# Two weight matrices turned by VectorE through DRAM, rows broadcast by DMA, and batch 0's projections in seven block products

## The chip, the cores and the metric

One core of one Trainium2 chip. The metric is the device time of one execution in microseconds (us). The engines are TensorE (PE, with its weight loads PEld), VectorE (DVE), ScalarE (ACT), GpSimd (POOL) and SyncE (SP, which here only issues DMAs). All data is float32. Each engine works through its own instructions in order and meets the others at semaphores.

## The reference

Sixteen batches of a graph with 1024 nodes and 256 channels pass two layers, each on the normalized and rectified input, with a residual:

```python
# layer 0
h = relu(layernorm(x))
c_adj = mean(h, axis=-1)                        # one value per node
A_s = 1 - |tanh((c_adj[m] - c_adj[n]) / 2)|     # the reference's A_s, in short
g = relu((h^T @ (adj * A_s)) * para)            # queries, 4 heads of 64
k, v = split(h @ kv_w)                          # kv_w: 256 x 512
x = x + softmax(q k^T * scale) @ v
# layer 1
h = relu(layernorm(x))
A_hat = (adj + I) * dinv[:, None] * dinv[None, :]   # dinv = rsqrt(degree)
z = batchnorm_relu((A_hat @ h) @ W1.T + b1)         # W1: 512 x 256
x = x + batchnorm(z @ W2.T + b2)                    # W2: 256 x 512
```

Both batchnorms take their statistics over all batches and nodes, so the second linear layer can only start when all sixteen batches have passed the first.

## The kernel before

[...] Wherever it can, the kernel forms a product of 2 x 2 blocks in seven block products instead of eight: sums of blocks are prepared, seven products are made, and the results are gathered by copies (ACT) and adds (DVE) out of PSUM.

The first stage runs batch by batch: `graph` (the weighted adjacency times h, then queries, keys and values), `attention` (four steps, each of scores, exponentials, sums and values), and then layer 1's aggregation and first linear product of the batch. Preparation of later batches is woven between by lists of steps: `between[c]` is called before block c of the graph, `hooks[s]` at the end of step s of attention. The order of PE, ACT, DVE, POOL and SP is the order of the program: a manual schedule. A DMA issued from SP or POOL waits in that engine's line like any other instruction.

PSUM is three double banks (`ps_s`) and two single ones (`ps_o`, `ps_t`). While a graph runs, two of the three double banks hold its sums (`gps`), and the third serves what is woven in. In attention `ps_o` holds the step's output; DVE turns it out of the bank (L874), and only then can the next step's values begin.

What lies around the change:

- Batch 0 and batch 1 use `graph` (plain products); from batch 2 on `graph_seven` is used, whose keys and values go through a class `Seven` in an order written out by hand. Its operands are sums of kv_w's blocks (made once by `make_key_sums`, stored in `kvs_d`, loaded for each batch) and sums of the turned h's blocks (`kt1` to `kt4`).
- Batch 0's h is turned by `turn_h` on SP's queue: DVE turns 32x32 blocks (L381), 32 small DMAs put them in place (L388).
- `prepare_row(b)` broadcasts batch b's sums of h over all partitions: by PE transposes for batches 0 and 1, through DRAM from batch 2 on (L310, L311).
- W1 is loaded with one DMA (L1408), turned by eight PE transposes (`turned`, L1378) and copied by ACT (L1412) into `w1T`, in `between[2]` of batch 0. `make_w1_sums` (L1095 to L1099) comes after batch 0's graph, then `make_key_sums`, `prepare_row(1)` and `diagonal`: POOL multiplies the diagonal blocks with the identity and adds it (L1348, L1349), and DVE reduces the products (L1350). Then comes attention of batch 0.
- The degree's row sums (L1335) run on ACT in `between[7]` and `between[8]` of batch 0; the column sums in the hooks of attention. `roots` (L1353 to L1355) makes `dinv`, `roots_row` (L1361, L1362) broadcasts it by PE transposes in `between[3]` of batch 1, and `scale_adj` (L1369) scales the turned adjacency with it: three rows in `between[4]`, one more behind it, four after the graph.
- W2 is loaded at the start of batch 15's attention (L1475), turned by eight PE transposes between its linear products (L1556) and copied by ACT (L1559).
- The pool `pp` has eight buffers with the tag "p". Exponentials of a step take all eight; the sums of W1, the diagonal's products, turned h and turned weights take one each while they live.

Of the kernel before, what the change touches and what calls it, by code (L numbers as in the profile page):

```python
# [10 lines left out]
F32 = mybir.dt.float32  # L11
# [6 lines left out]
P = 128  # L18
# [11 lines left out]
def fast_path(  # L30
# [37 lines left out]
    gs_d = [dram.tile([P, 4 * NC // 2, P], F32, tag=f"fgs_{b}", name=f"fgs_{b}") for b in range(B)]  # L68
    w1s_d = dram.tile([P, 4, FC * P // 2], F32, tag="fw1s", name="fw1s")
# [106 lines left out]
    with ExitStack() as stage:  # L176
# [126 lines left out]
        def prepare_row(b):  # L303
# [5 lines left out]
            if b > 1:  # L309
                nc.sync.dma_start(row_d[b].rearrange("(c p) -> p c", p=P), sums_of[b])  # L310
                nc.sync.dma_start(row, row_d[b].unsqueeze(0).to_broadcast([P, N]))  # L311
                return
# [6 lines left out]
            if b > 0:  # L319
                nc.scalar.copy(row, first)  # L320
                return


# [69 lines left out]

        def graph(b, between):
# [38 lines left out]
            for step in between.get("late", ()):  # L433
                step()
            for d in range(CC):
# [73 lines left out]
        def graph_seven(b, left, norm, load_more, last):  # L509
# [149 lines left out]
            t23 = ow.tile([P, 2, 512], F32, tag="sums", name=f"f_kt23_{b}")  # L659
            kt4 = pp.tile([P, 2, 512], F32, tag="acc", name=f"f_kt4_{b}", bufs=2)[:, 0]  # L660
            kt2, kt3 = t23[:, 0], t23[:, 1]
            part = lambda k, j: hT[k][:, ts(j, 512)]
            nc.vector.tensor_sub(kt3, part(1, 1), part(0, 1))
            nc.vector.tensor_add(kt2, kt3, part(0, 0))
            kt1 = part(0, 1)
            nc.vector.tensor_sub(kt1, kt1, part(0, 0))
            nc.vector.tensor_sub(kt4, part(1, 0), kt2)
# [10 lines left out]
            class Seven:  # L678


                def __init__(self, name, n, c, turned):
                    self.name, self.n, self.c, self.turned, self.ps = name, n, c, turned, {}
                    sums, o = (ps_s, "s"), (ps_o, "o")
                    self.banks = {
                        "x": sums,
                        2: (ps_t, "t"),
                        7: o if turned else sums,
                        4: sums if turned else o,
                    }

                def place(self, key, pool, tag):
                    ps = pool.tile([P, 512], F32, tag=tag, name=f"f_{self.name}ps{key}_{b}")
                    self.ps[key] = ps.rearrange("p (n q) -> p n q", n=4) if self.turned else ps

                def product(self, m):
                    w = lambda i, k: kvw_t[:, k, ts(2 * self.n + i, P)]
                    s = lambda q: sums[:, self.n, q]
                    left, right = {
                        1: (w(0, 0), part(0, 0)),
                        2: (w(0, 1), part(1, 0)),  # L700
                        3: (s(3), part(1, 1)),
                        4: (w(1, 1), kt4),
                        5: (s(0), kt1),
                        6: (s(1), kt2),
                        7: (s(2), kt3),
                    }[m]
                    more = m in (3, 5, 6)
                    key = "x" if more or m == 1 else m
                    if not more:
                        self.place(key, *self.banks[key])  # L710
                    ps = self.ps[key]
                    if not self.turned:
                        nc.tensor.matmul(  # L713
                            ps, left, right, start=not more, stop=True, skip_group_check=more
                        )
                        return
                    for n in range(4):
                        nc.tensor.matmul(  # L718
                            ps[:, n],
                            right[:, ts(n, P)],  # L720
                            left,
                            start=not more and n == 0,
                            stop=n == 3,
                            skip_group_check=True,
                        )

                def copy(self, i, j):
                    nc.scalar.copy(self.c(i, j), self.ps["x"])

                def add(self, i, j, m):  # L730
                    nc.vector.tensor_add(self.c(i, j), self.c(i, j), self.ps[m])  # L731

            V = Seven("v", 1, lambda i, j: v[:, 4 * j : 4 * j + 4, ts(i, P)], True)
            K = Seven("k", 0, lambda i, j: kT[:, i, ts(j, 512)], False)
# [366 lines left out]
        def make_key_sums():  # L1101
# [9 lines left out]
            nc.sync.dma_start(kvs_d, t)  # L1111

# [244 lines left out]
        def roots_row():  # L1357
            t = pp.tile([P, N], F32, tag="p", name="f_drow")
            ps = ps_s.tile([P, NC, P], F32, tag="s", name="f_drowps")
            for c in range(NC):  # L1360
                nc.tensor.transpose(ps[:, c, :], dinv[:, c : c + 1].to_broadcast([P, P]), ident)  # L1361
            nc.scalar.copy(  # L1362
                t.rearrange("p (i c q) -> p c i q", i=NC, c=NC),
                ps.rearrange("p c (q i) -> p c i q", i=NC),
            )
            drow.append(t)

        def scale_adj(m):
            nc.vector.scalar_tensor_tensor(  # L1369
                ahatT[:, m, :], ahatT[:, m, :], dinv[:, m : m + 1], drow[0], ALU.mult, ALU.mult  # L1370
            )

        def turned(src, n, k, name):

            ps = ps_s.tile([P, k, n, P], F32, tag="s", name=f"f_{name}ps")
            for d in range(k):
                for f in range(n):
                    nc.tensor.transpose(ps[:, d, f, :], src[:, f, ts(d, P)], ident)  # L1378
            return ps.rearrange("p d f q -> p (d f q)")

        with tc.manual_schedule(engines={ENG.PE, ENG.Activation, ENG.DVE, ENG.Pool, ENG.SP}):
# [25 lines left out]
            w1n = w4.tile([P, FC, C], F32, tag="w4", name="f_w1n")  # L1407
            nc.sync.dma_start(w1n, W1.rearrange("(f p) d -> p f d", p=P))  # L1408
            w1T = big.tile([P, CC, F1], F32, tag="w1T", name="f_w1T")

            def turn_w1():
                nc.scalar.copy(w1T.rearrange("p d f -> p (d f)"), turned(w1n, FC, CC, "w1"))  # L1412
# [13 lines left out]
                        turn_w1,  # L1426
# [13 lines left out]
                        lambda: place_adj_aside(6, nc.vector.tensor_copy),  # L1440
                    ],
# [4 lines left out]
                    6: [lambda: prepare_end(1), lambda: again(0)],  # L1446
                    7: [lambda m=m: row_sums(m) for m in range(4)],
                    8: [lambda m=m: row_sums(m) for m in range(4, NC)],
# [3 lines left out]
            make_key_sums()  # L1452
            prepare_row(1)
            diagonal()
            for b in range(B):

                hooks, aside, behind = {}, {}, None
                if b + 1 < B:
# [9 lines left out]
                    if b == 0:  # L1468
                        for m in range(NC):
                            hooks.setdefault(m // 2, []).append(lambda m=m: column_sums(m))  # L1470
                        hooks[3].append(roots)
# [989 lines left out]
```

## Time and profile before

| | |
|---|---|
| median of 3 runs | 2368.37 us (2367.6 to 2368.43) |
| the profiled execution | 2368.14 us, span 2366.4 us |
| TensorE's granted clock in it | 0.997 |
| batch 0: graph, then keys and values | 15.91 to 50.67, then to 64.45 us |
| batch 0: attention | 65.41 to 121.82 us |
| batch 1: graph, then keys and values | 121.75 to 150.20, then to 165.29 us |

The page gives the busy time of each engine, the span in slices, the chain of work that ended last, and the costliest groups. A timeline lists an engine's instructions: start, duration, engine, line, operation, what is written and read, how often, and in brackets how long the engine was idle before and what released it. A list of waits gives total time, times and the longest.

### The profile page before, as it was taken

The page shows a single profiled execution, that of the slowest core. Times are in us where ns is not written, and L with a number is a line of the kernel's source. Part 1 is how long each engine was busy: PE and PEld are TensorE (multiplying, and loading weights), DVE is VectorE, ACT ScalarE, POOL GpSimd, SP SyncE. Part 2 cuts the span into 40 slices and gives each one's busy share as a digit, 9 for nine tenths or more (in the row PEclk, how much of TensorE's full clock was granted, in tenths as well). Part 3 has the DMA queues.
Part 4 walks back from the last instruction along what each step waited for, and adds up shares of the span by engine and source line. Part 5 has one row for each costly group of instructions (what it writes and reads, how often), then busy time and mean ns, then how long its engine had stood idle before and what let it go on. Part 6 is the DMA issues. An engine that isn't in the chain of part 4 may idle for free.

```text
span 2366.4 us, 25724 instructions
## 1 busy us (share of the span) xinstructions
PE 2323.3 (98%) x8258; PEld 1031.8 (44%) x8258; DVE 1985.0 (84%) x2923; ACT 1418.6 (60%) x2057; POOL 441.2 (19%) x565
## 2 busy tenths in 40 slices
PE   8999999999999999999999999999999999999995
PEld 4443444434343434444343434344444434444444
DVE  6788989897989889897989798988989898757766
ACT  6846556574837465665748384746556575346644
POOL 2041212122221112221212221121212121100000
PEclk9999999999999999999999999999999999999998
DMA  5043343433342434434343424353353521355569
GB/s 189 17 135 106 134 142 116 149 118 116 115 145 78 170 98 148 128 122 155 109 128 128 134 79 162 89 178 98 134 142 116 160 72 54 124 213 180 173 239 379
DMA packets 167264, 323.78 MB, mean 137 GB/s; under 512 B 33616, under 2 KB 100688, under 8 KB 167120
## 3 DMA queue, kind: packets, MB, share of 16 engines
q1 hardware_dynamic: 143696, 266.44, 32.8%
q0 software_dynamic: 18816, 38.83, 6.1%
q10 hardware_dynamic: 4608, 16.78, 1.7%
q8 instruction: 67, 1.10, 0.2%
q14 instruction: 77, 0.63, 0.1%
HBM read 202.38 MB, written 100.72 MB: 128 GB/s over the span
## 4 chain that ended last, share of the span: by engine, by line
PE 94%; DMA 2%; DVE 1%; POOL 1%; issue 1%; ACT 0%; SPq 0%; DVEq 0%; ACTq 0%; POOLq 0%
PE f_s L809 19%; PE f_o L861 19%; PE f_aps L1026 16%; PE f_gps L571 8%; PE f_gpsx L571 6%; PE f_zps L1133 6%; PE f_zx L1683 4%; PE f_zm L1683 3%; PE f_vpsx L718 2%; PE f_kpsx L713 2%; PE f_vps L718 2%; PE f_kps L713 1%; PE f_gps L413 1%; DMA f_z<-fx 1%; PE f_vps L459 1%
## 5 line engine op out<-in xcount | busy, mean ns | idle before, releaser
L817 ACT ACTIVATE f_p<-f_s 128x1024 f32<-128x1024 f32 x512 | 477.1, 1045 | 61.4 <-PE f_s L809 61.3
L809 PE MATMUL f_s<-f_qT,f_kT 64*128 64x512 f32 x2048 | 457.1, 596 | 1.2 <-DVE f_kT L731 1.2
L861 PE MATMUL f_o<-f_p,f_v 128*64 128x512 f32 x2048 | 453.6, 595 | 0.0
L809 PEld LDWEIGHTS f_s<-f_qT,f_kT 64*128 64x128 f32 x2048 | 191.1, 185 | 264.6 <-issue 117.2
L861 PEld LDWEIGHTS f_o<-f_p,f_v 128*64 128x64 f32 x2048 | 141.4, 137 | 304.3 <-issue 265.6
L366 POOL TENSOR_TENSOR f_w<-f_w,f_adj 128x1024 f32<-128x1024 f32 x56 | 132.4, 2364 | 701.5 <-ACT f_w L365 528.7
L929 POOL DMA_DIRECT2D f_att<-f_oT x256 | 136.3, 540 | 381.2 <-DVE f_oT L912 374.4
L832 DVE TENSOR_TENSOR f_acc<-f_acc,f_p 128x1024 f32<-128x1024 f32 x128 | 155.7, 1217 | 4.6 <-ACT f_p L817 4.6
L832 DVE TENSOR_TENSOR f_sums<-f_sums,f_p 128x1024 f32<-128x1024 f32 x128 | 155.6, 1215 | 0.0
L353 ACT ACTIVATE f_w<-f_row,f_col 128x1024 f32<-128x1024 f32 x127 | 147.3, 1160 | 9.2 <-DMA f_row<-frow 6.6
L356 ACT ACTIVATE f_w<-f_w 128x1024 f32<-128x1024 f32 x127 | 134.3, 1058 | 4.0
L1026 PE MATMUL f_aps<-f_ahatT,f_hs 128*128 128x512 f32 x256 | 115.1, 592 | 0.0
L1026 PE MATMUL f_aps<-f_ahatT,f_h_b 128*128 128x512 f32 x256 | 112.7, 593 | 0.1
L1026 PE MATMUL f_aps<-f_t,f_hs 128*128 128x512 f32 x256 | 112.5, 592 | 0.0
L365 ACT ACTIVATE f_w<-f_w,f_now 128x1024 f32<-128x1024 f32 x56 | 64.3, 1149 | 80.1 <-DVE f_now L363 80.1
L571 PE MATMUL f_gps<-f_w,f_h_a 128*128 128x512 f32 x224 | 109.9, 592 | 0.0
L823 DVE TENSOR_TENSOR f_acc<-f_p,f_p 128x1024 f32<-128x1024 f32 x64 | 77.9, 1217 | 31.7 <-ACT f_p L817 31.7
L281 ACT ACTIVATE f_h_a<-f_x,f_shift_a,f_rstd_a 128x256 f32<-128x256 f32 x126 | 73.8, 587 | 39.5 <-DVE f_shift_a L266 39.4
L829 DVE TENSOR_TENSOR f_sums<-f_p,f_p 128x1024 f32<-128x1024 f32 x64 | 78.1, 1220 | 21.8 <-ACT f_p L817 21.8
L370 DVE SCALAR_TENSOR_TENSOR f_w<-f_w,f_adj 128x1024 f32<-128x1024 f32 x71 | 88.0, 1256 | 8.0 <-ACT f_w L356 8.0
L281 ACT ACTIVATE f_h_b<-f_x,f_shift_b,f_rstd_b 128x256 f32<-128x256 f32 x128 | 66.2, 590 | 28.6 <-DVE f_shift_b L266 28.6
L1156 ACT ACTIVATE f_z<-f_zps,f_b 128x512 f32<-128x512 f32 x60 | 38.0, 684 | 75.2 <-PE f_zps L1133 75.2
(298 smaller groups left out, 3971.8 us busy)
## 6 DMA issues: line engine op xcount, KB each, us to landing
f_t<-ft SPq DMA_DIRECT2D x84, 512.0 KB, 9.7
fz<-f_z SPq DMA_DIRECT2D x64, 512.0 KB, 9.7
f_x<-in_x_dram SPq DMA_DIRECT2D x31, 1024.0 KB, 6.1
f_zb<-fz SPq DMA_DIRECT2D x42, 512.0 KB, 4.4
fx<-f_x SPq DMA_DIRECT2D x16, 1024.0 KB, 4.4
fgs<-f_gs POOLq DMA_DIRECT2D x28, 512.0 KB, 3.0
fhT<-f_hQ POOLq DMA_DIRECT2D x112, 128.0 KB, 3.2
f_hT<-fhT SPq DMA_DIRECT2D x28, 512.0 KB, 6.3
```

Of the source, the lines that this page charges most:

```text
L281: nc.scalar.activation(self.h[:, c, :], self.xt[:, c, :], AF.Relu, bias=self.shift[:, c : c + 1], scale=self.rstd[:, c : c + 1], accum_out ...
L353: nc.scalar.activation(w, rows[b], AF.Abs, bias=cols[b][:, c : c + 1], scale=0.5 / C)
L356: nc.scalar.activation(w, w, AF.Tanh)
L571: nc.tensor.matmul(ps, left, right, start=fresh and n == 0, stop=(n == PAIRS - 1), skip_group_check=more,)
L809: nc.tensor.matmul(ps[:, e, :], kT[rows_e, pair, ts(m, P)], qT[rows_e, pair, ts(g, 512)], start=True, stop=True,)
L817: nc.scalar.activation(p, ps, AF.Exp)
L832: nc.vector.tensor_add(to, to, p)
L861: nc.tensor.matmul(o_of[s][e * HD : (e + 1) * HD, :], v[:, m, ts(2 * pair + e, HD)], p[:, e, :], start=(m == 0), stop=(m == NC - 1),)
L929: queue.dma_start(t[ts(j, 32), :, a].rearrange("r h c i -> r h (c i)"), oT[ts(a, 32), :, j].rearrange("r h c i -> r h (c i)"),)
L1026: nc.tensor.matmul(ps, left[:, m, :], right(m), start=not more and m == 0, stop=(m == KH - 1), skip_group_check=more,)
L1133: nc.tensor.matmul(ps[i], left[:, ts(i, P)], right, start=not more, stop=True, skip_group_check=more,)
L1683: nc.tensor.matmul(ps, left[:, m, :], right[:, m, :], start=start and m == 0, stop=(m == 1), skip_group_check=not start,)
```

## The change

- W1 and W2 are loaded with four DMAs each (`load_rows`), turned in 32x32 blocks by DVE and stored by four POOL DMAs in DRAM (`turn_weights`); `w1T` and `w2T` are loaded from there by SP. W2 is handled right after batch 0's graph, between the W1 sums and the diagonal.
- `roots_row` stores `dinv` in DRAM with a POOL DMA and loads it broadcast, at the end of step 3 of batch 0's attention. The row is now in natural order, and `scale_adj` reads it with a step of eight elements.
- Batch 1's row of sums goes through DRAM as the later ones do.
- Batch 0's keys and values use `Seven`, moved out of `graph_seven`, with an order of its own; the key sums are made before, in `between[6]`, and kept in SBUF.
- The row sums move to `between[4]`; batch 1's row, the key sums and the load of `w1T` move into `between[6]`.

```diff
+            if b == 0:
+                part, kt = h_sums(b, hT)
+                V, K = projections(b, kT, v, part, kt, key_sums[0])
+                V.product(1)
+                V.copy(0, 0)
+                for d in range(CC):
+                    nc.vector.tensor_mul(qT[:, d, :], gps[d], para_t[d])
+                V.product(2)
+                V.add(0, 0, 2)
+                K.product(1)
+                K.copy(0, 0)
+                V.product(6)
+                V.copy(1, 0)
+                V.product(7)
+                K.product(2)
+                K.add(0, 0, 2)
+                V.product(5)
+                V.copy(1, 1)
+                V.add(1, 0, 7)
+                V.add(1, 1, 7)
+                K.product(6)
+                K.copy(1, 0)
+                V.product(4)
+                V.add(1, 0, 4)
+                V.product(3)
+                V.copy(0, 1)
+                K.product(5)
+                K.copy(1, 1)
+                K.product(7)
+                K.add(1, 0, 7)
+                K.add(1, 1, 7)
+                K.product(4)
+                K.add(1, 0, 4)
+                for d in range(CC):
+                    nc.scalar.activation(qT[:, d, :], qT[:, d, :], AF.Relu, scale=-SCALE)
+                K.product(3)
+                K.copy(0, 1)
+                return qT, kT, v
...
+        def h_sums(b, hT):
+            t23 = ow.tile([P, 2, 512], F32, tag="sums", name=f"f_kt23_{b}")
+            kt4 = pp.tile([P, 2, 512], F32, tag="acc", name=f"f_kt4_{b}", bufs=2)[:, 0]
+            kt2, kt3 = t23[:, 0], t23[:, 1]
+            part = lambda k, j: hT[k][:, ts(j, 512)]
+            nc.vector.tensor_sub(kt3, part(1, 1), part(0, 1))
+            nc.vector.tensor_add(kt2, kt3, part(0, 0))
+            kt1 = part(0, 1)
+            nc.vector.tensor_sub(kt1, kt1, part(0, 0))
+            nc.vector.tensor_sub(kt4, part(1, 0), kt2)
+            return part, (kt1, kt2, kt3, kt4)
...
         def roots_row():
             t = pp.tile([P, N], F32, tag="p", name="f_drow")
-            ps = ps_s.tile([P, NC, P], F32, tag="s", name="f_drowps")
-            for c in range(NC):
-                nc.tensor.transpose(ps[:, c, :], dinv[:, c : c + 1].to_broadcast([P, P]), ident)
-            nc.scalar.copy(
-                t.rearrange("p (i c q) -> p c i q", i=NC, c=NC),
-                ps.rearrange("p c (q i) -> p c i q", i=NC),
+            nc.gpsimd.dma_start(dinv_d.rearrange("(c p) -> p c", p=P), dinv)
+            nc.sync.dma_start(t, dinv_d.unsqueeze(0).to_broadcast([P, N]))
+            drow.append(t)
+
+        def scale_adj(m):
+            at = ahatT[:, m, :].rearrange("p (i q) -> p i q", i=NC)
+            nc.vector.scalar_tensor_tensor(
+                at,
+                at,
+                dinv[:, m : m + 1],
+                drow[0].rearrange("p (q i) -> p i q", i=NC),
+                ALU.mult,
+                ALU.mult,
             )
...
+        def load_rows(w, n, name):
+            t = w4.tile([P, N], F32, tag="w4", name=f"f_{name}n").rearrange("p (n d) -> p n d", n=n)
+            rows = w.rearrange("(a n r) d -> a r n d", a=4, n=n)
+            for a in range(4):
+                nc.sync.dma_start(t[ts(a, 32)], rows[a])
+            return t
+
+        def turn_weights(src, out, n, name):
+            k = N // (n * P)
+            t = pp.tile([P, k, 4, n, 32], F32, tag="p", name=f"f_{name}Q")
+            nc.vector.transpose(
+                t.rearrange("p k q n r -> p n (k q) r"),
+                src.rearrange("p n (k i) -> p n k i", i=32),
+            )
+            to = out.rearrange("(q i) k m -> i k q m", q=4)
+            for a in range(4):
+                nc.gpsimd.dma_start(
+                    to[:, :, :, ts(a, 32 * n)], t[ts(a, 32)].rearrange("i k q n r -> i k q (n r)")
+                )
...
                         lambda: weights(0, 4),
-                        turn_w1,
+                        lambda: turn_weights(w1n, w1T_d, FC, "w1"),
...
+                        *(lambda m=m: row_sums(m) for m in range(NC)),
...
-                    6: [lambda: prepare_end(1), lambda: again(0)],
-                    7: [lambda m=m: row_sums(m) for m in range(4)],
-                    8: [lambda m=m: row_sums(m) for m in range(4, NC)],
+                    6: [
+                        lambda: prepare_end(1),
+                        make_key_sums,
+                        lambda: prepare_row(1),
+                        load_w1T,
+                        lambda: again(0),
+                    ],
                 },
             )
             make_w1_sums()
-            make_key_sums()
-            prepare_row(1)
+            turn_weights(load_rows(W2, CC, "w2"), w2T_d, CC, "w2")
             diagonal()
...
-                        hooks[3].append(roots)
+                        hooks[3].extend([roots, roots_row])
                 else:
                     hooks[0] = [lambda norm=norm: norm.relu(0, NC, False)]
-                    w2n = lasting.tile([P, CC, F1], F32, tag="w2n", name="f_w2n")
-                    nc.sync.dma_start(w2n, W2.rearrange("(c p) f -> p c f", p=P))
+                    w2T = lasting.tile([P, FC, C], F32, tag="w2T", name="f_w2T")
+                    nc.sync.dma_start(w2T, w2T_d)
```

## The prediction

> **What bounds the kernel now.** I read the page first: busy time by engine, and the chain that ended last.
>
> ```profile
> span 2366.4 us, 25724 instructions
> PE 2323.3 (98%) x8258; PEld 1031.8 (44%) x8258; DVE 1985.0 (84%) x2923; ACT 1418.6 (60%) x2057; POOL 441.2 (19%) x565
> PE 94%; DMA 2%; DVE 1%; POOL 1%; issue 1%; ACT 0%; SPq 0%; DVEq 0%; ACTq 0%; POOLq 0%
> ```
>
> TensorE (PE) is the bound: work taken from it is time gained, unless it then waits. So next, who made PE wait, in the whole span:
>
> ```profile
> PE f_adjps L1308 <- DMA f_adj<-in_adj_dram: 9.6, 1, 9.6
> PE f_kps L439 <- DVE f_qT L430: 1.0, 1, 1.0
> PE f_w1ps L1378 <- DMA f_w1n<-in_L_gnn_W_dram: 0.8, 1, 0.8
> ```
>
> Only the last two are near the change. Then the timelines of single engines around the edits (start, duration, line, operation, count, idle before):
>
> ```profile
> 54.44 0.33 SPq L1099 DMA_DIRECT2D fw1s<-f_w1s  x1
> 50.99 0.54 POOL L1348 TENSOR_TENSOR f_unused_d<-f_ahatT,f_ident 128x128 f32<-128x128 f32 x1 [18.77 <-ACT f_unused_r L1335]
> 60.01 1.22 DVE L1350 TENSOR_REDUCE f_diag<-f_unused_d 128x8 f32<-128x1024 f32 x1 [1.56 <-POOL f_unused_d L1348]
> 65.41 7.14 PE L809 MATMUL f_s<-f_qT,f_kT 64*128 64x512 f32 x32
> 68.62 1.23 DVE L823 TENSOR_TENSOR f_acc<-f_p,f_p 128x1024 f32<-128x1024 f32 x1 [7.39 <-ACT f_p L817]
> 70.45 1.23 DVE L829 TENSOR_TENSOR f_sums<-f_p,f_p 128x1024 f32<-128x1024 f32 x1 [0.61 <-ACT f_p L817]
> 81.04 0.71 DVE L874 STREAM_TRANSPOSE f_oT<-f_o 128x512 f32<-128x512 f32 x1
> 86.56 7.09 PE L861 MATMUL f_o<-f_p,f_v 128*64 128x512 f32 x32
> ```
>
> Each engine follows program order: VectorE (DVE) stood 1.56 us at the diagonal's reduction until GpSimd (POOL) had multiplied, and SP's store at L1099 waited 7.3 us for the W1 sums (waits of the SP queue). Today this costs nothing: DVE is idle 7.39 us before attention's first add. In attention, values(1) at 86.56 writes the bank that DVE empties at 81.04+0.71 = 81.75: a margin of 4.8 us, plus the 0.61 of idle at 70.45. DVE may start attention 5.4 us late, no more.
>
> **Up to the end of batch 0's graph.** Eight W1 transposes leave PE (25.67 to 26.57, 0.9) with their 0.8 wait. But the next transposes need the banks that DVE empties in its copies from 24.72 and 25.32 (L1329, 0.68 each, end 26.00). So graph block 2 starts at 26.5, not 27.44: −0.94 of 1.7. DVE gets one 128x1024 block transpose, 1.18 (half of L381's 2.37), before batch 1's statistics; what PE needs of DVE next is the emptied banks at 35.19 (in hand since 31.69), so 1.2 is covered; uncovered it costs at most 1.2. W1's four loads fall in SP's idle stretch (5.0 us before L388), its four stores (0.56 each) in POOL's (20.16 us). The row sums move into ACT's 7.73 us idle ahead of batch 1's ReLU: 8 x 1.04 from 32.6 to 40.9, when its shift is ready. The eight key sums (54.34 to 58.05, 3.7) fill DVE's 7.29 us idle before L430. The four sums of h (0.69 each, L663 to L667 in batch 2) need the last of SP's 32 turns of h (issued 43.2, 1.9 to land): 45.1 to 48.6, ahead of PE at 49.73. All at nothing.
>
> **Keys and values.** Now 50.67 to 64.45: 13.78. Seven products each take 0.86 (keys) and 0.89 (values, turned), as in batch 2 (281.91 to 294.25, no PE wait): 12.25. −1.53. Following every copy (0.59), add (0.69) and bank through the written order I find no PE wait; the one that a key product's add causes today, before the last batch's scores, is 1.2 (f_s on L731), and that is the bound here.
>
> **Batch 1's row.** Eight transposes leave, −0.96 (64.45 to 65.41). The store and broadcast load queue on SP behind the key sums' store: stored at about 46, landing 4.3 to 13.1 (frow in later batches), loaded some 6 us later, by 65; ACT wants it after 70. At nothing. [...]
>
> So scores of batch 0 start at 65.41 − 0.94 − 1.53 − 0.96 = 61.98.
>
> **What stands behind W2's turn.** After batch 0's keys and values come, in program order: W1 sums (DVE) and their store (SP), W2's four loads (SP), its turn (DVE), four stores (POOL), the diagonal's 16 operations (POOL), its reduction (DVE), attention. A chain across three queues, where POOL ran the diagonal early before:
> - DVE ends the last key add at 62.3 (PE's product 4 of the keys ends 61.12), W1 sums to 64.7 (2.4, as 52.02 to 54.42).
> - SP can't load W2 before the sums' store: 0.33, then four issues near 0.5; the last is issued at 66.5. Landing: 1.9 (32 KB on SP) to 4.1 (256 KB); I take 3.0, since 512 KB stores here took 2.6: 69.5.
> - DVE turn 1.18 (at most 1.25): 70.7.
> - POOL wakes 0.36 after it (as at L504; 0.6 at most), four stores of 0.56 (0.50 to 0.82, the columns at the start): 73.3.
> - Diagonal to the reduction: 9.0 (50.99 to 60.01); with POOL's fastest spacing of a pair, 1.08, it is 8.1: 82.3.
> - Reduction 1.14: attention's first add at 83.4 instead of 61.98+3.21 = 65.2.
>
> Of the pairs on POOL, those beside DVE's sums came 1.1 to 1.34 apart, the last, beside an idle DVE, 1.08. [...]
>
> DVE needs 81.75 − 68.62 − 0.61 = 12.5 from the first add to emptying the bank: 95.9. PE would be at values(1) at 61.98+21.15 = 83.1. **PE stands 12.8 us** (10.6 with all low ends, 15.4 with all high). Queued behind the late reduction are all adds of attention, which also hold the p buffers; so exponentials of step 1 are late too, by my count ready a little before 95.9.
>
> **Graph of batch 1.** Eight root transposes leave (0.87), for nothing: PE's 1.0 wait at L439 ends a chain that starts at DVE's turn of h after attention, runs through POOL's 32 + 8 DMA issues (124.81 to 145.94) and ends with the query product at 153.57, and PE only waits longer. DVE also comes 4.8 − 3.56 = 1.2 later relative to PE, 3.56 being its idle time in steps 1 to 3 which it can use up: +1.2 (0.6 to 1.2). The roots' store and load have some 15 us before the first scaling. Scaling now reads the row in steps of 8 elements; no row shows that from SBUF. The copies at L1314, which read PSUM so, take 1.22, like plain ones: I take nothing; were each of the last four twice as long, 4 x 1.22 − 0.3 (PE's margin at 172.15) = +4.6.
>
> **W2 in batch 15.** Eight transposes leave (0.87), but PE's next work at 2066.08 waits for the bank that DVE empties at 2066.03 (L1189), and DVE is held by POOL's power (shift at 2063.40), not by PE: −0.1 (0 to −0.87).
>
> **Sum.** −3.43 + 12.8 + 1.2 − 0.1 = +10.5 on the span, 2376.9; 1.74 lies around the span (2368.14 for the profiled run), so 2378.6. The median of the runs shown is 0.23 above it, inside their spread. Low ends 10.6, 0.6, −0.87: +6.9 (2375.0); high ends 15.4, 1.2, 0, and −2.5 if the early gain fails: +14.1 (2382.2); the strided scaling would lie beyond.
>
> **Rivals.**
> - W2's loads don't wait for the W1 sums' store (3.0+1.8 earlier): first add at 78.6, PE stands 8.0, sum +5.7: 2374. Against it: the 7.3 us wait at L1099. 0.09.
> - The other side: POOL does the diagonal outside W2's line, or DVE's reduction ends by 61.98+3.21+5.4 = 70.6; from there down PE doesn't stand, and −3.43 − 0.1 stay: 2364.6, within 0.2%. If PE also keeps the roots' and W2's 0.87 each: 2363.0. For it: W2's data is wanted only in batch 15. Against: the diagonal is written after the turn. 0.14 (0.07 each).
> - Strided scaling at twice the time, or a p buffer held longer than I count: 2381 to 2387. 0.07.
>
> **Chances.** Main case 0.70. A measurement of this kernel tells 0.2%, 4.7 us, from no change. The main case, the first rival and the third are slower: 0.82 after some loss at the first one's edge; the second gives 0.07 faster, and 0.11 remain within. Range 2370 to 2384; the main case alone 2375 to 2382.
>
> **What would show it.** Right: scores of batch 0 start near 62; DVE idle some 4 to 5 us before W2's turn (released by a DMA) and some 12 at L1350's reduction (released by POOL); PE waiting some 13 us in all in attention 0 for DVE or for exponentials; L439's wait 2 to 3 us. Wrong: a reduction of the diagonal before 71, PE waits in keys and values of batch 0, scaling above 1.3 us.

## The result, and the profile after

| | before | after |
|---|---|---|
| median of 5 runs, us | 2368.43 (2367.60 to 2368.82) | 2391.86 (2391.12 to 2393.89) |
| ratio | | 1.0101, 95% interval [1.0087, 1.0116] |
| span of the profiled execution, us | 2366.4 | 2391.5 |

The change makes the kernel 23.4 us slower by the medians (the profiled execution of it took 2393.33 us, 1.5 above its median). The page of the changed kernel, busy time by engine; then its list of PE's waits (total us, times, longest), which answer to the lines shown of before:

```profile
span 2391.5 us, 25768 instructions
PE 2328.7 (97%) x8248; PEld 1031.6 (43%) x8248; DVE 1997.5 (84%) x2937; ACT 1416.4 (59%) x2056; POOL 447.0 (19%) x574
```

```profile
PE f_o L912 <- ACT f_p L868: 11.2, 2, 6.2
PE f_kps L554 <- DVE f_qT L507: 9.5, 1, 9.5
...
PE f_aps L1077 <- DVE f_z L1243: 0.9, 1, 0.9
PE f_o L912 <- DVE f_oT L925: 0.9, 1, 0.9
```

PE is still the bound, and it has three new stalls: 12.1 us in batch 0's attention (L912, three waits; the stage as a whole grows by 15.6), 9.5 us ahead of batch 1's second key product (L554, 1.0 before), and 0.9 in batch 15 where W2's transposes were. Lengths of stages, read from PE's timelines, add up to the whole difference of 25.1 us of span:

| stage | before | after | difference | predicted |
|---|---|---|---|---|
| to batch 0's scores | 65.41 | 62.46 | -2.95 | -3.43 |
| attention of batch 0 | 56.34 | 71.96 | +15.62 | +12.8 |
| graph of batch 1, to its second key product | 33.09 | 40.70 | +7.61 | +1.2 |
| from there to batch 1's scores | 46.59 | 49.73 | +3.14 | 0 |
| the rest | 2164.97 | 2166.65 | +1.68 | -0.1 |

**Attention.** The chain that ended last, between 40 and 100 us (start, duration, what):

```profile
47.59 10.27 DMA frow<-f_sums
...
58.39 7.65 DMA f_w1T<-fw1T
...
69.81 3.27 DMA f_w2n<-in_L_gnn_W_dram
...
74.75 0.78 POOL fw2T L1446
```

This is the line that the prediction drew (W1 sums, W2's load, turn, stores, diagonal, reduction), with two links ahead of it that it did not draw: the 10.27 us store of batch 1's row and W1's 7.65 us load. The timeline of DVE, with what ended its idle time in brackets, dates it:

```profile
66.07 0.42 DVE L1146 TENSOR_TENSOR f_w1s<-f_w1T 128x256 f32<-128x256 f32 x1 [3.26 <-DMA f_w1T<-fw1T]
...
73.21 1.25 DVE L1440 STREAM_TRANSPOSE f_w2Q<-f_w2n 128x1024 f32<-128x1024 f32 x1 [5.59 <-DMA f_w2n<-in_L_gnn_W_dram]
85.73 1.22 DVE L1404 TENSOR_REDUCE f_diag<-f_unused_d 128x8 f32<-128x1024 f32 x1 [11.27 <-POOL f_unused_d L1402]
86.86 1.22 DVE L874 TENSOR_TENSOR f_acc<-f_p,f_p 128x1024 f32<-128x1024 f32 x1
```

The waits are 12.1 us and the stage is 15.6 longer because PE, when it does work inside the stall, works at half clock: the granted clock is 0.50 from 81.0 to 92.0 us, and a set of scores (from 90.01) takes 8.31 us instead of 7.14. What ends the stall is DVE's turn of the bank at 98.48, so this half clock costs nothing more.

**Graph of batch 1.** The timeline of POOL shows the turns of h (L386) behind the store of the roots, and why GpSimd stood between them:

```profile
134.90 0.95 POOL L1413 DMA_DIRECT2D fdinv<-f_dinv  x1 [0.29 <-POOL f_dinv L1409]
137.96 3.50 POOL L386 DMA_DIRECT2D f_hT<-f_hQ  x7 [2.11 <-issue]
144.18 3.90 POOL L386 DMA_DIRECT2D f_hT<-f_hQ  x8 [2.72 <-DMA fdinv<-f_dinv]
150.54 4.44 POOL L386 DMA_DIRECT2D f_hT<-f_hQ  x9 [2.46 <-DMA f_hT<-f_hQ]
```

Before, all 32 went out in one stretch of 15.72 us. Now the ninth DMA of GpSimd waits until the first, the store, has landed (9.0 us), and later ones for turns that take 5.8 us instead of 1.8. What PE then waits for is not the turned h itself: the first key product, which reads it, starts at 162.00 without a wait. It is DVE's query product, at the end of this chain:

```profile
144.66 5.82 DMA f_hT<-f_hQ
...
161.12 3.69 POOL f_att L980 x7
...
170.32 3.42 POOL f_rstd_b L263
...
173.84 1.23 DVE f_qT L507
```

Behind the turns in GpSimd's line stand the stores of batch 0's attention output (L980, at 141.72 before); from that output comes the power that GpSimd takes for batch 0's next normalisation (L263), then DVE's shift, and behind the shift, in DVE's order, the query product.

**After the wait.** Windows of the same trace: from and to, length, busy time and instructions of PE, PEld, DVE, ACT and POOL, granted TensorE clock, DMA share, GB/s:

```profile
175.00:177.00 2.00, 1.88 (x3) 0.85 (x4) 2.00 (x3) 2.00 (x6) 0.00 (x0) 0.50 0.00 0
177.00:179.00 2.00, 2.00 (x4) 0.97 (x3) 2.00 (x2) 2.00 (x5) 0.00 (x0) 0.50 0.00 0
179.00:181.00 2.00, 2.00 (x3) 0.71 (x3) 2.00 (x2) 0.86 (x1) 0.00 (x0) 0.50 0.78 218
181.00:183.00 2.00, 2.00 (x9) 1.39 (x8) 2.00 (x2) 1.16 (x2) 0.00 (x0) 0.96 0.87 306
```

PE is busy but at half its clock for 6 us: the eight matmuls of the key product take 6.69 us instead of 3.70.

### The profile page after: what moved, and what is told of

Same layout as the page of the kernel before. It is cut to its first block, busy times and chain, and to the rows that moved or that the text cites. A ratio compares the mean times of both kernels' runs of the same rounds, so it can differ in the third digit from the quotient of the medians.

```text
span 2391.5 us, 25768 instructions
## 1 busy us (share of the span) xinstructions
PE 2328.7 (97%) x8248; PEld 1031.6 (43%) x8248; DVE 1997.5 (84%) x2937; ACT 1416.4 (59%) x2056; POOL 447.0 (19%) x574
## 4 chain that ended last, share of the span: by engine, by line
PE 88%; DVE 3%; DMA 3%; issue 2%; ACT 1%; POOL 1%; SPq 0%; DVEq 0%; POOLq 0%; ACTq 0%
PE f_s L860 17%; PE f_o L912 17%; PE f_aps L1077 16%; PE f_gps L686 8%; PE f_zps L1187 6%; PE f_gpsx L686 6%; PE f_zx L1740 4%; PE f_zm L1740 3%; PE f_vpsx L434 2%; PE f_kpsx L429 2%; PE f_vps L434 1%; PE f_kps L429 1%; DMA f_z<-fx 1%; PE f_outps L1958 1%; PE f_z2ps L1678 1%
## 5 line engine op out<-in xcount | busy, mean ns | idle before, releaser
L912 PE MATMUL f_o<-f_p,f_v 128*64 128x512 f32 x2048 | 455.8, 597 | 12.1 <-ACT f_p L868 11.2
L912 PEld LDWEIGHTS f_o<-f_p,f_v 128*64 128x64 f32 x2048 | 141.4, 137 | 318.0 <-issue 262.2
L980 POOL DMA_DIRECT2D f_att<-f_oT x256 | 136.2, 539 | 368.2 <-DVE f_oT L963 342.7
```

What stands on the lines that cost most here:

```text
L912: nc.tensor.matmul(o_of[s][e * HD : (e + 1) * HD, :], v[:, m, ts(2 * pair + e, HD)], p[:, e, :], start=(m == 0), stop=(m == NC - 1),)
L980: queue.dma_start(t[ts(j, 32), :, a].rearrange("r h c i -> r h (c i)"), oT[ts(a, 32), :, j].rearrange("r h c i -> r h (c i)"),)
```

## The experiments

Lengths of stages are from each run's profile; times are medians, beside the kernel before on the same chip (2368.07 to 2368.49).

### Which part costs what: W2, the roots, the rest

Three kernels undo W2, the roots, or both.

```diff
-            turn_weights(load_rows(W2, CC, "w2"), w2T_d, CC, "w2")
...
-                    w2T = lasting.tile([P, FC, C], F32, tag="w2T", name="f_w2T")
-                    nc.sync.dma_start(w2T, w2T_d)
+                    w2n = lasting.tile([P, CC, F1], F32, tag="w2n", name="f_w2n")
+                    nc.sync.dma_start(w2n, W2.rearrange("(c p) f -> p c f", p=P))
```

> W2 is loaded and turned as in the kernel before (TensorE, in batch 15); the rest of the change stays. My theory: the line W1 sums, W2's load, turn and stores, diagonal, reduction costs attention of batch 0 15.6 us (71.96 instead of 56.34 us from its scores to the end). Without it the diagonal runs early on GpSimd, and attention takes 56 to 57 us again: 2391.9 - 15.6 = about 2376; the later losses (batch 1's graph, +7.6, its key product, +3.1) stay. Rival A: the late W1 load behind the row's store (3.3 us) or p buffers held by the other new stores keep PE standing without W2: attention stays above 62 us and the time above 2381. Rival B: the later losses follow from attention's delay too: below 2370.

Measured 2375.59 us, ratio 1.0031 [1.0019, 1.0043]. Attention lasts 56.34 us as before, though DVE still waits 4.66 us for W1's load; that lateness alone is inside the prediction's 5.4 us of slack. The wait at L554 stays (8.25 us). My theory holds.

```diff
-            nc.gpsimd.dma_start(dinv_d.rearrange("(c p) -> p c", p=P), dinv)
-            nc.sync.dma_start(t, dinv_d.unsqueeze(0).to_broadcast([P, N]))
+            for c in range(NC):
+                nc.tensor.transpose(ps[:, c, :], dinv[:, c : c + 1].to_broadcast([P, P]), ident)
...
```

(The scaling reads contiguous operands again, too.)

> Batch 1's roots go through TensorE as in the kernel before, with the contiguous scaling; W2 stays early. My theory: the roots' 4-byte store on GpSimd's queue blocks the turns of h behind it. Without it PE's wait for the query product ahead of batch 1's second key product falls from 9.5 to about 1 to 2 us, that key product runs at a full clock again (eight matmuls in about 3.7 instead of 6.7 us), and the eight transposes come back (+0.9): 2391.9 - 8 - 3 + 0.9 = about 2381. Rival A: DVE is late out of attention anyway, and the roots' store only fills that: wait of 6 us or more, 2388 to 2391. Rival B: the strided scaling alone matters (4 x 0.8 us): 2388 to 2389.

Measured 2384.12 us, 1.0065 [1.0050, 1.0081]; attention 72.75 us. PE's line there, with the wait and the product at full clock:

```profile
168.61 3.70 PE L554 MATMUL f_kps<-f_hT,f_kvw 128*128 128x512 f32 x8 [1.51 <-DVE f_qT L507]
```

The roots cost 7.7 us by the medians, less than the 11 that I wrote; 0.8 of the gap is attention, which came out longer in this profile.

Both edits together:

> W2 and batch 1's roots as in the kernel before; what is left of the change: W1 turned through DRAM, batch 1's row of sums through DRAM, seven products for keys and values of batch 0. My theory: the two losses are separate, and what is left gains the 2.95 us by which batch 0's scores start earlier, against W1's turn on DVE (nothing): about 2365 (2364 to 2367). Rival: something else of the change costs too (W1's turn, the row's store), so 2369 or more.

Measured 2366.68 us (11 runs), 0.9994 [0.9985, 1.0004], within the range that I wrote. Against it, W2 costs 17.4 us (2384.12) and the roots 8.9 (2375.59); both together 25.2 (2391.86), so they are nearly separate. What is left of the change gains 1.4 us by the medians, and the interval includes no gain.

And with the row and W1 undone too, so that the seven products are all that is left of the change:

```diff
-            if b > 0:
+            if b > 1:
                 nc.sync.dma_start(row_d[b].rearrange("(c p) -> p c", p=P), sums_of[b])
...
-                        lambda: turn_weights(w1n, w1T_d, FC, "w1"),
+                        turn_w1,
```

> The kernel before, with the seven block products for batch 0's keys and values alone; W1, W2, batch 1's row and roots go through TensorE as before. Prediction's term: 12.25 instead of 13.78 us, 1.5 us less: 2366.9. Rival: the DVE work of the recombination (a key add ahead of the last batch's bank) makes PE wait, and nothing is gained: 2368.4.

Measured 2367.36 us, 0.9996 [0.9987, 1.0005]. In the trace the seven products take 12.27 us, 0.02 from the predicted 12.25, but the wait at the second key product grows from 1.05 to 1.53: a third of the gain is given back there.

### Attention: which link of the line

```diff
-            turn_weights(load_rows(W2, CC, "w2"), w2T_d, CC, "w2")
             diagonal()
+            turn_weights(load_rows(W2, CC, "w2"), w2T_d, CC, "w2")
```

> The change as it is, but the diagonal is written ahead of W2's turn, so GpSimd multiplies it early as before. My theory: the length of the whole line counts, W2's landing included: DVE now stands only at W2's turn (to about 74), its first add comes near 75 instead of 86.9, and exponentials wait for the p buffers that W2's tiles hold: PE stands some 5 to 8 us instead of 15.6: 2382 to 2387. Rival A: GpSimd's 8 us of diagonal are all of it, since 75 is only 4 us past the point from which DVE is late: PE stands no more, 2376 to 2378. Rival B: the p buffers held by W2's stores decide and the diagonal nothing: 2390 to 2392.

Measured 2380.44 us, 1.0050 [1.0034, 1.0065], between my range and rival A. DVE's first add comes at 74.79, as written, but attention lasts only 59.4 us: PE waits 2.15 us in two waits, since exponentials were held 3.79 us, not to the end of W2's stores. GpSimd's 8 us of diagonal behind the turn is the largest link; W2's landing alone still costs 3 us.

```diff
                         make_key_sums,
+                        lambda: w2n.append(load_rows(W2, CC, "w2")),
                         lambda: prepare_row(1),
```

> The change as it is, but W2's four loads are issued before batch 1's row is stored, not behind the W1 sums. Theory A: the line then begins when DVE is free after the W1 sums: the turn of W2 about 5 us earlier, the first add of attention at about 81.5 instead of 86.9, PE stands some 5 us less: 2386 to 2387. Theory B: GpSimd's stores and diagonal begin no earlier, as another wait takes that place: 2391 to 2392.

Measured 2388.30 us, 1.0085 [1.0070, 1.0101]: 3.6 us less than the change, between the two theories. The turn now follows the W1 sums without a wait, but the sums start 2.7 us later: the row's store now goes out behind W2's loads and takes 11.4 us, and W1's load, behind both, is issued at 60.92 instead of 58.39.

```diff
+                        load_w1T,
                         lambda: prepare_row(1),
-                        load_w1T,
```

> The change as it is, with one swap in SP's line: the turned W1 is loaded before batch 1's row of sums is stored and loaded, not behind it. Theory A: the row's 4-byte store (10.3 us to land) held W1's load, the W1 sums started 3.3 us late, and the whole line of W2 with them: DVE's first add of attention comes 24.4 - 3 = about 21.4 us after batch 0's scores begin (the prediction's own figure), attention is 2.8 us shorter, 2389 us. Theory B: DVE or another DMA sets that start: no change, 2391 to 2392.

Measured 2394.34 us, 1.0108 [1.0091, 1.0125]: my theory fell in this form. The W1 sums start at 62.51, right behind the last key add, but W2's turn begins no earlier:

```profile
73.79 1.25 DVE L1440 STREAM_TRANSPOSE f_w2Q<-f_w2n 128x1024 f32<-128x1024 f32 x1 [9.73 <-DMA f_w2n<-in_L_gnn_W_dram]
```

W2's loads took 7.5 us to land instead of 3.3. As the row's store lands (12.6 us after its issue), SP lets go the row's 512 KB and 1 MB of x at once, and W2's loads come behind them. In the change it was W1's load that the store held: it was issued at 58.39 instead of 45.81 here, and took 7.65 us against 7.0. So the row was taken out of SP's line:

```diff
-            if b > 0:
+            if b > 1:
                 nc.sync.dma_start(row_d[b].rearrange("(c p) -> p c", p=P), sums_of[b])
...
```

> The change as it is, but batch 1's row of sums goes through TensorE as in the kernel before (eight transposes, +0.96 us), so neither its store nor its load is in SP's line. Theory A: the transfers released as the row's store lands (the row's 512 KB and the next batch's 1 MB of x) are what makes W1's or, after the swap, W2's load late; without the row's store they are out of the way, W2's turn begins about 21.4 - 13.2 = 8.2 us after batch 0's scores instead of 10.75 us, attention is 2.5 to 3.5 us shorter than 71.96 us, and the time is 2.5 to 3.5 less and 0.96 more: about 2390. Theory B: attention as long as in the change, 2393.

Measured 2388.42 us (2388.36 to 2392.27), 1.0086 [1.0070, 1.0103]. The W1 sums at 62.98, W2's turn at 70.11 [5.51 <- its load], attention 67.8 us: 4.1 us shorter for 0.96 us of transposes. The row's pair of DMAs, not the order of the loads, made the line late.

### The roots: the queue, the load, or the pieces

```diff
-            nc.gpsimd.dma_start(dinv_d.rearrange("(c p) -> p c", p=P), dinv)
+            nc.sync.dma_start(dinv_d.rearrange("(c p) -> p c", p=P), dinv)
```

> W2 as before (so that attention is undisturbed); the roots go through DRAM as in the change, but their store is issued by SP instead of GpSimd. Theory A: the store's 9.0 us on GpSimd's queue hold the turns of h behind it (GpSimd's ninth DMA waited until it had landed). On SP it holds nothing there: PE's wait for the query product falls from 9.5 to 2 to 4 us, and the time is 6 to 9 us below the kernel with W2 alone as before, near 2367 to 2370. Theory B: the traffic that the store and its 512 KB load bring in slows the turns of h on whatever queue: the wait stays above 7 us and the time within 2 us of that kernel.

Measured 2378.85 us, 1.0046 [1.0030, 1.0061]; theory A fell: the wait is 9.69 us. Theory B held in the wait, not in the time, which is 3.3 us above the kernel with W2 alone as before instead of within 2. The DMAs from 123 to 134 us in this run: GB/s in 40 slices of 0.275 us, and the turns issued (KB each, median us to landing). The store, issued on SP at 120.68, took 12.3:

```profile
GB/s 0 0 0 0 0 0 0 52 67 82 37 112 8 119 37 82 60 60 104 15 119 0 0 0 0 0 0 0 0 0 0 0 0 0 0 0 0 0 0 0
...
f_hT<-f_hQ POOLq DMA_DIRECT2D x10, 32.0 KB, 7.7
```

In this run the first turns, on another queue than the store, land with it. By these records the store does not keep the DMA engines busy for so long: its 1040 packets all lie before 123, those of the first eight turns end at about 128.8, and from there to 134 nothing is moved, though the store lands only at 133.0 and the first turn at about 133.4. Theory B blamed the traffic of store and load together, so the two were tried apart, each added to the kernel with both parts as before (nothing reads the result of either):

```diff
-                        hooks[3].append(roots)
+                        hooks[3].extend(
+                        [
+                            roots,
+                            lambda: nc.gpsimd.dma_start(
+                                dinv_d.rearrange("(c p) -> p c", p=P), dinv
+                            ),
+                        ]
+                    )
```

> The kernel with W2 and the roots as before (2366.7), with the roots' store in 1024 pieces on GpSimd's queue added; nothing reads it. Theory A (the pieces): the turns of h are late as in the change, PE's wait for the query product grows from 0.5 to 6 us or more, and the key product is slow: 2373 to 2376. Theory B (the load): the store alone costs its 0.95 us of issue at most: 2367 to 2369.

```diff
-                        hooks[3].append(roots)
+                        hooks[3].extend(
+                        [
+                            roots,
+                            lambda: nc.sync.dma_start(
+                                pp.tile([P, N], F32, tag="p", name="f_drow2"),
+                                row_d[1].unsqueeze(0).to_broadcast([P, N]),
+                            ),
+                        ]
+                    )
```

> The kernel with W2 and the roots as before (2366.7), with one more 512 KB broadcast load (of batch 1's row of sums) issued on SP where the store of the roots stands in the change; nothing reads it. Theory A (the pieces): a load of 4 to 6 us delays a few turns at most: PE's wait 0.5 to 2 us, 2366 to 2369. Theory B (the load): the wait is 6 us or more and the time 2372 or more.

The store alone: 2372.13 us, 5.5 more than without; the wait at L554 is 4.25 us and the product takes 5.97 (4.25 and 2372.13 are a little less than the 6 us and the 2373 that I wrote for theory A). The load alone: 2366.23 us, no cost, wait 0.64 (it was issued at 114.75, away from the turns). So the store's 4 KB, not the load's 512, is the head of it; the other 3.4 us of the roots' 8.9, by the difference, come only with both. That they are the load's, which then follows the late store into the turns, is argued and not tested. The last test keeps everything and changes the pieces:

```diff
-            nc.gpsimd.dma_start(dinv_d.rearrange("(c p) -> p c", p=P), dinv)
+            nc.gpsimd.dma_start(dinv_d.rearrange("(p c) -> p c", p=P), dinv)
...
-                t.rearrange("p (i q) -> p i q", i=NC),
-                drow[0].rearrange("p (q i) -> p i q", i=NC),
+                t.rearrange("p (i c s) -> p i c s", i=NC, c=NC),
+                drow[0].rearrange("p (s i c) -> p i c s", i=NC, c=NC),
```

> As the kernel with the plain scaling, but the roots are stored in 128 pieces of 32 bytes (a partition's eight side by side) instead of 1024 of 4 bytes; ScalarE's reordering copy reads the row in the matching order. Theory A: the many pieces hold the DMA engines, and the turns of h behind them land late; with 128 pieces the store lands in 2 to 3 us instead of 9.0, PE's wait falls from 7.95 to 1 to 2.5 us and the key product runs in 3.7 us: 2375.6 - 6 - 1.7 = about 2368 (2366 to 2369). Theory B: the 512 KB load behind the store does it: the wait stays above 6 us and the time at 2374 to 2376.

Measured 2367.02 us (11 runs), 0.9994 [0.9985, 1.0003]: 8.6 us less for 128 pieces of 32 bytes instead of 1024 of 4. Its POOL timeline and its DMAs:

```profile
120.22 0.61 POOL L1413 DMA_DIRECT2D fdinv<-f_dinv  x1 [0.29 <-POOL f_dinv L1409]
123.28 15.64 POOL L386 DMA_DIRECT2D f_hT<-f_hQ  x32 [2.45 <-issue]
```

```profile
f_hT<-f_hQ POOLq DMA_DIRECT2D x32, 32.0 KB, 1.8
...
fdinv<-f_dinv POOLq DMA_DIRECT2D x1, 4.0 KB, 1.8
```

The store lands in 1.8 us, the 32 turns go out without a wait, and the load, issued at 122.14 and landing in 3.9 us, does no harm that the medians tell (2367.02 us against 2366.68 with the roots on TensorE). PE's wait falls to 1.89 us, as written; the key product, expected in 3.7 us, takes 5.40, at half clock for most of it (0.50 from 155 to 157 us). This settles it: the pieces, though the empty slices above speak against theory A's reason, that they hold the DMA engines.

### The strided scaling and the clock

```diff
-                drow[0].rearrange("p (q i) -> p i q", i=NC),
+                drow[0].rearrange("p (i q) -> p i q", i=NC),
```

(with one ScalarE copy that orders the row first, W2 as before.)

> W2 as before; the roots' row lands as in the change and ScalarE first copies it into the permuted order, so that DVE scales batch 1's graph with contiguous operands (1.22 us each) instead of steps of 8 elements (2.0 us each). Theory A: the slower scaling is hidden, since PE's slow second key product of batch 1 (6.7 us for eight matmuls) gives DVE the time: the time is within 1 us of the kernel with W2 alone as before. Theory B: the four last scalings are on PE's path: 3 us less.

Measured 2375.57 us, the same as 2375.59: with the roots' stall in place the slower scaling (8.08 us for the last four, 4.86 before) is hidden.

> The kernel before, with one thing of the change: batch 1's scaling reads the roots' row in steps of 8 elements. Theory A: each scaling takes 2.0 instead of 1.22 us, and with a key product at full clock (3.7 us) nothing hides the four last: PE waits some 2.5 to 3 us for them, 2371 (ratio 1.001). Theory B: DVE's time is hidden here too: 2368.4.

Measured 2372.41 us, 1.0020 [1.0011, 1.0029]: without the roots' stall it costs 4.3 us. PE's waits:

```profile
155.74 3.70 PE L439 MATMUL f_kps<-f_hT,f_kvw 128*128 128x512 f32 x8 [2.14 <-DVE f_qT L430]
176.13 7.10 PE L1026 MATMUL f_aps<-f_t,f_hs 128*128 128x512 f32 x16 [2.92 <-DVE f_hs L1011]
```

2.92 was expected; the 1.1 more at the query product (2.14 instead of 1.05) I had missed: one scaling stands ahead of it.

```diff
+                if d == 1:
+                    idle = ps_t.tile([P, 512], F32, tag="t", name="f_idle")
+                    for n in range(10):
+                        nc.tensor.matmul(
+                            idle, kvw_t[:, 0, 0:P], hT[0][:, 0:512], start=True, stop=True
+                        )
```

> As the kernel with the plain scaling, and PE gets ten more 512-column matmuls, whose result nothing reads, in its wait ahead of batch 1's second key product. Theory A: the idle stretch of 9.5 us is what lowers the granted clock (0.50 after it): with PE busy there the eight matmuls of that product take 3.6 to 4.2 us instead of 6.7, and the time falls by up to 3 us. Theory B: the clock falls for another reason, or the product is slow for its data: it takes 6 us or more, and the time is the same.

Measured 2373.41 us (10 runs), 1.0023 [1.0014, 1.0032]: 2.2 us less with more work on PE.

```profile
159.06 3.60 PE L560 MATMUL f_kps<-f_hT,f_kvw 128*128 128x512 f32 x8
```

The product is at full clock again (granted 1.00 from 155 to 163 us; without the ten it took 5.37 us, behind a wait of 7.95). Between these two runs the idle stretch is what slows it.

The half clock and the strided scaling hide each other. In all eight profiles with the strided scaling and the shift in its place, the stage from the second key product to batch 1's scores lasts 49.69 to 49.75 us, whether the product takes 3.70 us (the kernel before with the strided scaling) or 6.77; where it ends sooner, PE waits longer for DVE's sums of h (1.00 us behind a product of 5.56, none behind 6.69). With the plain scaling the stage follows the product: 46.49 us at full clock, 48.25 behind a product of 5.37. So in the change either of the two alone would make nearly all of the 3.1 us of this stage: the scaling alone made 3.2 in the kernel before, and a product of 6.69 us is 3.0 longer than one of 3.70.

### A version below both

Batch 0's shift, the last link but one of the chain above, for which DVE waits on GpSimd's power ahead of the query product, is written behind batch 1's queries:

```diff
+                    between["queries"] = between.pop(6) + between.pop("late")
```

> W2 and the roots as before, and batch 0's shift of a normalisation is written behind batch 1's queries, so that DVE does not stand at GpSimd's power (3.4 us) ahead of the query product. Theory A: PE's wait of 1.0 us ahead of batch 1's second key product goes: 1 us below the kernel with both as before, about 2364. Theory B: PE waits for the turns of h all the same, or the late shift holds batch 0's ReLU: no gain, or a loss of 1 to 3 us.

> The kernel with the roots in 128 pieces, and batch 0's shift written behind batch 1's queries. If the store in pieces no longer delays the turns, this has the roots' eight transposes (0.87) less than the kernel with the late shift and the roots on TensorE (2365.2): about 2364.5. If DVE still waits for the turns of h, the shift's move gains less than 1 us: 2366 to 2368. If the pieces are not the cause: above 2372.

Both measured 2365.18 us (11 runs each): 0.9985 [0.9976, 0.9994] with the roots on TensorE, 0.9988 [0.9979, 0.9997] with the roots in 32-byte pieces. In both PE no longer waits at the second key product. They are 3.2 us below the kernel before, about 1 above what I wrote. The shift's own part, 1.5 and 1.8 us by the medians, is too small for these intervals to show, and the roots' eight transposes are worth nothing that these runs can tell.

## Why the prediction was wrong

The direction and the main mechanism were right (slower, by W2's line in attention); 2391.86 us lies 7.9 us above the range's end. Of the 14.6 us of span that the sum lacks, 6.4 arise in the graph of batch 1, 3.1 in the stage behind it, 2.8 in attention.

- **To batch 0's scores**: predicted -3.43, measured -2.95. From the end of PE's first wait for a DMA (9.64 and 9.35 us) to the first product of keys or values it is 41.03 us before and 40.45 after: -0.58 instead of -0.94. From there to the scores 14.74 and 12.66: -2.08 instead of -2.49; 12.25 of products had been counted, and 0.4 of small gaps stand between them. The remaining -0.29 is the first wait itself, which these changes don't touch.
- **Attention**: right in kind, 2.8 us too small. "At nothing", I wrote of the row's store and load on SP, because ACT wants the row late. I had not asked what SP issues behind them: W1's load stands there, and the W1 sums began 3.3 us late. (The "4.3 to 13.1" that the prediction gives for the landing of such a store mixes two kinds of transfer: 4.3 is the shortest of the row's 512 KB loads, and the fourteen stores in the trace of before took 8.5 to 13.1.) Without the row's DMAs attention is 67.8 us, where the prediction's own sum makes 69.1. The other links came as worked out: W1 sums 2.4 predicted and 1.6 measured, landing of W2 3.0 and 3.3, turn 1.18 and 1.25, stores 2.24 and 2.98, diagonal 9.0 and 8.0; DVE's two waits, 4 to 5 and some 12 in the prediction, are 5.59 and 11.27. PE's waits for exponentials and its half clock lie inside the stall, and DVE's turn at 98.48 ends it, as written. The first two rivals (W2's loads free of the W1 sums' store; the diagonal outside the line) did not occur.
- **Graph of batch 1**: this is the step that failed. The DVE part, 1.2, was right: with the roots undone the stage is 33.56 us, 1.0 longer than with W2 undone as well. But "the roots' store and load have some 15 us before the first scaling" priced a moved step by its consumer alone. The store holds the turns of h, on GpSimd's queue (later turns take 5.8 us to land instead of 1.8) and beside it (with the store on SP ten of them took 7.7 by the median), and those turns are the start of the very chain that the prediction had drawn for L439's wait, through GpSimd's 32 + 8 DMA issues to the query product: the stage is 40.70 us with it, 7.1 more. The wait foretold as 2 to 3 us is 9.5.
- **The key product after the wait**: not in the sum at all. It takes 6.69 us at half clock instead of 3.70, and the stage is 3.1 longer; the strided scaling alone would make it as long.
- **Strided scaling**: taken at 1.22, measured 2.02; "scaling above 1.3 us" was one of the prediction's own signs of being wrong. It was priced among the rivals (+4.6 at twice the time). In the change the half clock hides it; without the stall it costs 4.3.
- **W2 in batch 15**: -0.1 predicted; a wait of 0.94 took the place of 0.87 of transposes. Right.
- The rest, +1.7, was not traced; in the profiles of the experiments the same stretch varies from 2164.3 to 2168.6 us.

The prediction had set down how long such a store takes to land for the row (4.3 to 13.1 us), and set down nothing for the roots, whose store took 9.0. Why turns on another queue land with the store, and why DVE takes 2.02 us instead of 1.22 where the row is read in steps of eight elements, no run here shows.

## What to carry to other kernels

Price a moved DMA by what stands behind it, on its issuer's queue and on the other queues, not only by who reads it; and look at how many pieces it is cut into before its bytes (4 KB landed in 9.0 us as 1024 pieces, in 1.8 as 128). Where a new wait is put on PE, look for a slow clock after it (0.50 here after one of 9.5 us). A cost that seems hidden may be hidden by another cost (the strided scaling: nothing behind the roots' stall, 4.3 us without it): undo one, and it appears.

## What the runs showed of the hardware

A store of 4 KB in 4-byte pieces took 8.5 to 13.1 us to land in these traces (the later batches' rows included), in 32-byte pieces 1.8 us. Beside one on SP's queue, which took 12.3, ten turns on GpSimd's queue landed after 7.7 us by the median, instead of 1.8.

The clock after a wait does not follow from the wait's length alone. After 1.89 us it fell in one run, after 2.14 us it stayed full in another. Windows of the kernel with the 32-byte pieces, then of the kernel before with the strided scaling:

```profile
151.30:153.20 1.90, 0.08 (x1) 0.00 (x0) 1.29 (x3) 1.09 (x3) 0.58 (x1) 1.00 0.00 0
153.20:155.00 1.80, 1.73 (x3) 0.83 (x4) 1.80 (x3) 1.80 (x5) 0.00 (x0) 0.77 0.00 0
155.00:157.00 2.00, 2.00 (x4) 0.84 (x3) 2.00 (x3) 2.00 (x5) 0.00 (x0) 0.50 0.00 0
157.00:159.00 2.00, 2.00 (x7) 0.99 (x6) 2.00 (x2) 1.31 (x3) 0.00 (x0) 0.85 0.71 213
```

```profile
153.50:155.70 2.20, 0.10 (x1) 0.00 (x0) 1.32 (x3) 1.11 (x3) 0.85 (x1) 1.00 0.00 0
155.70:157.00 1.30, 1.26 (x3) 0.68 (x4) 1.30 (x2) 1.30 (x3) 0.00 (x0) 1.00 0.00 0
```

Read from the shares, with the clock taken as either 1.00 or 0.50, the slow stretch of the first began at about 154.2, when PE was already busy again, and ended at about 157.6, 3.4 us later. What sets that length, and why the clock fell after 1.89 us of waiting in one run and not after 2.14 in another, no run here shows.
